# Time attention's scores in another order with the output behind them, and half of the band blocks whole

## The chip, the cores and the metric

The kernel runs on one core of one Trainium2 chip. The metric is the device time in microseconds (us). In the profile PE is TensorE's matmuls, PEld its weight loads, DVE VectorE, ACT ScalarE, POOL GpSimd, SP the engine that issues most DMAs.

## The reference, cut to what matters

```python
B, T, FB, C = (2, 256, 128, 128); H_T, H_F, BAND = (4, 4, 16)      # 4 heads of 32
xt = ln(x).transpose(0, 2, 1, 3)
x = x + mha(xt, t_wi, ..., causal_mask(T)).transpose(0, 2, 1, 3)   # over time
x = x + mha(ln(x), f_wi, ..., band_mask(FB, BAND))                 # over the 128 bands, |i - j| <= 16
x = x + gelu(ln(x) @ w1.T + b1) @ w2.T + b2                        # 128 -> 512 -> 128
# mha: softmax(q @ k.T / sqrt(32) + mask) @ v per head, then @ wo.T + bo
```

All in fp32, and each fp32 product (a matmul of the program) stands in the trace as two weight loads and two matmul records.

## The kernel before

**Tiling.** The work is cut into groups of four tiles of 128 rows by 128 channels: 128 groups `OverTime` (two sequences of 256 times each), then 128 `OverBands` (four times of 128 bands) and 128 `FeedForward`, in runs of eight of each in turn. Scores and weights are kept with keys on the partitions and queries along the free dimension. TensorE is used in tiles: `product` cuts a product of 128 columns into four of 32 columns (128\*32 in the profile), and scores use 32 rows (one head) by 64 columns (half of a tile's keys), 32\*64. There are so eight lanes (head, half) for scores and four column lanes for the rest.

**Order.** `run` walks over steps n and writes each engine's instructions in an order by hand; `InOrder` pins it. A step of the time stage holds pieces of several groups. On TensorE these are: the scores (`time_scores`), made up of the second tiles of group n (`second_scores`) and the first tiles of group n+1 (`first_scores`); `weigh` of group n-1, first the row sums rp (product with ones), then the weighted values op; `output` of group n-2 (yp = oT times the output weights); `queries_keys` and `values` of group n+2. ACT takes the exponentials of the scores (`second_weights`, `first_weights`) head by head, then `root_in_bank`, the two steps of `invert` on rp, two more exponentials, and copies q, k and v. DVE does `statistics`, `normalize` and `turn` (a 32x32 transpose, whose result goes through DRAM: four writes, `turned`, and one read a step later, `fetch`) of later groups, then `refine`, `finish` (adds yp to the residual, and issues the stores on SP at every second group) and `divide` (three instructions; the last makes oT). POOL masks and adds the weights.

**Banks.** [...] In the time stage they have names: first scores of head h go to a0 to a3, second scores to b0 to b3. When the exponentials have read them, the products of the same step take them: before, rp takes b0, op b3, yp a1, q a2, k b1 and v b2 (`Attention.place`, L1094). At the step's end the names are handed on in a cycle (L1167): of the banks just filled, a1 (yp) stays a1, b0 (rp) becomes a0, b1 (k) a3, and b3 (op) b1; q's stays a2 and v's b2. A score has to wait till the bank's last reader is done.

**Scores.** A first tile's keys face 256 queries; half 0 of them (e = 0) is multiplied with 256 columns, half 1 with 192 (the rest is masked). A second tile's keys face 128: 128 columns for one half and 64 for the other. The order before goes by pairs: for each (head, kind, sequence) both halves. The band scores (`OverBands.scores`) go block by block, half by half, head by head: 32 products of 64 keys by 80 queries a group.

Of the kernel before, what the change touches and what calls it, by code (L numbers as in the profile page):

```python
# [19 lines left out]
P = 128  # L20
H = 4
D = 32
BAND = 16
EPS = 1e-5
NEG = -1e38
NT = 4
# [6 lines left out]
HALF = P // 2  # L33
# [613 lines left out]
def rows_of(h):  # L647
    return slice(h * D, (h + 1) * D)
# [9 lines left out]
class OverTime(Attention):  # L658
# [16 lines left out]
        self.p1 = path.work.tile([P, 2, H, 2, P], F32, name="p1", tag="h", bufs=2)  # L675
        self.s1 = {h: path.bank([P, 2, P], "sp", path.banks[f"b{h}"]) for h in range(H)}

    def first_scores(self, h, s):
        r, a = rows_of(h), 2 * s * P
        for e in range(0, P, HALF):  # L680
            self.path.tensor.matmul(
                self.s0[h][e : e + HALF, s, e:], self.kT[r, a + e : a + e + HALF], self.qT[r, a + e : a + 2 * P],
                start=True, stop=True,
            )

    def second_scores(self, h, s):
        r, a = rows_of(h), (2 * s + 1) * P
        for e in range(0, P, HALF):
            q = P - HALF - e
            self.path.tensor.matmul(  # L690
                self.s1[h][e : e + HALF, s, q:], self.kT[r, a + q : a + q + HALF], self.qT[r, a + q : a + P],
                start=True, stop=True,
            )

    def first_weights(self, heads):
        for h in heads:
# [41 lines left out]
        self.rp = rp.rearrange("p s n q -> p (s n q)")  # L738


def time_scores(old, new):


    if new is not None:
        new.first_tiles()
    if old is not None:
        old.second_tiles()
    for h, second, s in (
        (0, 1, 0), (1, 0, 0), (2, 0, 0), (3, 1, 0), (0, 1, 1), (3, 1, 1), (0, 0, 0), (3, 0, 0),
        (1, 0, 1), (2, 0, 1), (0, 0, 1), (3, 0, 1), (1, 1, 0), (2, 1, 0), (1, 1, 1), (2, 1, 1),  # L750
    ):
        if second and old is not None:
            old.second_scores(h, s)
        if not second and new is not None:
            new.first_scores(h, s)


class OverBands(Attention):
# [5 lines left out]
    def scores(self, heads):  # L764
        path = self.path
        self.sp = {h: path.bank([P, NT * P], "sp") for h in heads}
        for i in range(NT):
            for e in range(2):
                keys = slice(e * HALF, (e + 1) * HALF)
                a = i * P + e * (HALF - BAND)  # L770
                q = slice(a, a + HALF + BAND)
                for h in heads:
                    r = rows_of(h)
                    path.tensor.matmul(
                        self.sp[h][keys, q], self.kT[r, i * P + e * HALF : i * P + (e + 1) * HALF], self.qT[r, q],
                        start=True, stop=True,
                    )

    def first_function(self):
# [107 lines left out]
class BoundedPath:  # L887
# [170 lines left out]
    def run(self, x, out):  # L1058
        groups = list(self.groups(x, out))

        def do(n, *names):
            if 0 <= n < len(groups):
                for name in names:
                    getattr(groups[n], name)()

        def at(n, kind):
            return 0 <= n < len(groups) and isinstance(groups[n], kind)

        def do_at(n, kind, *names):
            if at(n, kind):  # L1070
                do(n, *names)


        run0 = [i for i in range(len(groups)) if at(i, OverBands)][: RUN // NT]
        due = dict(zip(run0, (-5, -4, -4, -3, -1, 0, 1, 2)))
        due = {n: [i for i in run0 if run0[0] + due[i] == n] for n in range(-12, len(groups) + 2)}
        A = RUN // NT

        self.scalar.preload_act_table_set(EXP_SET)
        for n in range(-12, len(groups) + 2):  # L1080
            feeds = [at(n - 2 + i, FeedForward) for i in range(5)]
            bands = [at(n - 2 + i, OverBands) for i in range(5)]
            turn = feeds[2] and bands[1]
            old, new = (groups[i] if at(i, OverTime) else None for i in (n, n + 1))
            if bands[2] and feeds[1]:
                self.scalar.preload_act_table_set(EXP_SET)
            do_at(n + 4, FeedForward, "root")
            do(n, "first_half", "first_function", "first_mask")
            if n >= 0:
                do_at(n + 5, OverTime, "statistics")  # L1090
            if old is not None or new is not None:
                time_scores(old, new)
                b = self.banks
                Attention.place = dict(rp=b["b0"], op=b["b3"], yp=b["a1"], qp=b["a2"], kp=b["b1"], vp=b["b2"])  # L1094
            else:
                Attention.place = {}
            if old is not None:
                old.second_weights(old.late)
            if new is not None:
                new.first_weights(new.early[:1])  # L1100
            if old is not None:
                old.second_weights(old.early)
                old.mask_second()
                old.add(0)
                old.add(1)
            if new is not None:
                new.first_weights(new.early[1:])
            if n >= 0:
                do_at(n + 5, OverTime, "root_in_bank")
            if turn:  # L1110
                do(n, "second_half", "second_function")
            do_at(n + 3, OverTime, "fetch")
            do_at(n + 2, (OverBands, FeedForward), "fetch")

            for i in (2 * n + 12, 2 * n + 13) if n < -2 else (n + 10,) if n < 2 else ():
                if i >= NT:
                    do(i, "load")
            if n < -8 or n >= 0:
                do(n + 12, "load")
            if n >= 0:  # L1120
                for i in due[n]:
                    do(i, "statistics")
            do_at(n + 3, (OverBands, FeedForward), "normalize", "turn")
            do_at(n + 4, OverTime, "normalize", "turn")
            if n >= 0:
                do_at(n + 5, OverTime, "refine")
            if n < 0:
                do(n + 5, "statistics")
            do_at(n + 5, FeedForward, "statistics")
            if n == -4:  # L1130
                self.fold_rest()
                self.warm()
            do(n - 1, "weigh")
            do(n - 1, "invert_exactly" if turn else "invert")
            if new is not None:
                new.first_weights(new.late)
            if bands[2] or turn or old is not None:
                do(n - 2, "output", "finish")
            do(n - 1, "divide")
            if not turn:  # L1140
                do(n, "second_half", "second_function")
            if n in run0:
                do(n, "bias")
            if not bands[2] and old is None:
                do_at(n, FeedForward, "bias")
                do_at(n + A, OverBands, "bias")
                if at(n - 1, FeedForward) and at(n - 2, OverBands):
                    do_at(n + A - 1, OverBands, "statistics", "root")
                if not turn:
                    do_at(n + A, OverBands, "statistics", "root")  # L1150
            do_at(n + 2, OverTime, "queries_keys", "take_query", "take_key")
            do_at(n + 1, OverBands, "queries_keys", "take_query", "take_key")
            if n < 0:
                do_at(n + 5, OverTime, "root_by_scalar", "refine")
            for i in due[n]:
                do(i, "root_by_scalar", "refine")
            do_at(n, OverTime, "bias")
            if new is not None:
                new.mask_first()
            if not bands[2] and not turn and old is None:  # L1160
                do(n - 2, "output", "finish")
            do_at(n + 2, OverTime, "values", "take_values")
            do_at(n + 1, OverBands, "values", "take_values")
            if old is not None or new is not None:

                b = self.banks
                self.banks = dict(  # L1167
                    a1=b["a1"], a2=b["a2"], b0=b["a0"], b3=b["a3"], a0=b["b0"], a3=b["b1"], b1=b["b3"], b2=b["b2"]
                )


# [67 lines left out]
```

## Time and profile before

| | us |
|---|---|
| median of 3 runs (2706.91 to 2709.16) | 2707.29 |
| the profiled execution's own time | 2709.79 |
| its span | 2708.0 |
| busy PE / DVE / POOL / ACT in the span | 2670.3 / 2176.8 / 1952.8 / 1858.2 |

The span is the time from the first to the last instruction of the profiled execution. Busy time is the time in which at least one instruction of the engine is under way by its record; a matmul's end is modelled, so on PE the distance from start to start says more than busy time. In the lines of groups, the columns are: line, engine, operation, out<-in, tile rows\*columns, shape, count, then busy us, mean ns of one, idle us before it and who ended it. Every operation goes through one helper, so all have its line, L882. Timeline lines give the start, the duration, and the merged instructions.

The granted TensorE clock is full throughout. The time stage takes up the first 970 us or so, the bands and the feed-forward the rest.

### The profile page before, as it was taken

To read this page: it belongs to the slowest core of one execution; us is meant where nothing else is said; L and a number is where in the kernel's file an instruction comes from. 1 tells how busy PE (TensorE), PEld (TensorE's weight loads), DVE (VectorE), ACT (ScalarE), POOL (GpSimd) and SP (SyncE) were. 2 spreads that over 40 slices of the span, in tenths; PEclk is the share of its full clock that TensorE was granted. 3 is DMA by queue.
4 is the path that set the end of the run, shared out by engine and by line. 5 is a ranking of instruction groups with operands and counts; after the bars stand their busy time and mean duration, and the time that the engine had idled before them with its cause. 6 is when DMAs were issued, how large, how long until landed. Compare 5 with 4: busy or idle time off the path is not lost.

```text
span 2708.0 us, 156754 instructions
## 1 busy us (share of the span) xinstructions
PE 2670.3 (99%) x68662; PEld 1826.6 (67%) x68662; DVE 2176.8 (80%) x6708; ACT 1858.2 (69%) x3620; POOL 1952.8 (72%) x2297
## 2 busy tenths in 40 slices
PE   8999999999999999999999999999999999999998
PEld 5766666666766666666666666666666667666665
DVE  7888888888888898868779678687697796886974
ACT  6888888888888874755746647557456465575563
POOL 4888888888888887667657666676576666665762
PEclk9999999999999999999999999999999999999999
DMA  5555555555555535445454454454444444544533
GB/s 147 152 148 145 149 148 141 150 146 146 150 141 149 145 95 137 109 117 135 106 127 124 114 130 110 120 133 111 124 126 113 124 118 120 130 113 123 128 100 82
DMA packets 471513, 347.10 MB, mean 128 GB/s; under 512 B 43297, under 2 KB 405153, under 8 KB 470817
## 3 DMA queue, kind: packets, MB, share of 16 engines
q1 hardware_dynamic: 469568, 335.92, 48.2%
q8 instruction: 540, 8.85, 1.5%
q14 instruction: 157, 1.28, 0.2%
q10 hardware_dynamic: 1248, 1.05, 0.1%
HBM read 169.03 MB, written 167.77 MB: 124 GB/s over the span
## 4 chain that ended last, share of the span: by engine, by line
PE 81%; DVE 14%; DMA 2%; issue 1%; SPq 1%; ACT 0%; DVEq 0%; ACTq 0%
PE bank L882 81%; DVE xh L882 3%; DVE bank L882 3%; DVE z L882 2%; DVE stats L882 2%; DVE u L882 2%; DVE x L882 1%; DMA xnT<-turned 1%; DVE mv L882 1%; DMA turned<-z 1%; SPq L882 1%; DMA x<-in_x 0%; DVE oT L882 0%; DMA rows_sb<-in_rows 0%; ACT p L882 0%
## 5 line engine op out<-in xcount | busy, mean ns | idle before, releaser
L882 ACT ACTIVATE hT<-bank,b 128x512 f32<-128x512 f32 x512 | 347.0, 688 | 535.8 <-PE bank L882 517.7
L882 POOL TENSOR_SCALAR_AFFINE_SELECT pf<-pf 128x512 f32<-128x512 f32 x768 | 478.6, 637 | 248.1 <-ACT pf L882 221.7
L882 DVE TENSOR_SCALAR xh<-x,mv,rstd 128x160 f32<-128x160 f32 x1536 | 596.9, 431 | 14.3
L882 PEld LDWEIGHTS bank<-w2T_sb,hT 128*32 128x32 f32 x16384 | 459.7, 110 | 63.3 <-issue 39.7
L882 PE MATMUL bank<-xnT,wf 128*32 128x512 f32 x4096 | 489.1, 592 | 2.5 <-ACT p L882 2.5
L882 PE MATMUL bank<-w2T_sb,hT 128*32 128x128 f32 x16384 | 477.7, 273 | 1.1 <-issue 0.8
L882 PE MATMUL bank<-xnT,w1f 128*32 128x512 f32 x4096 | 474.8, 592 | 0.0
L882 DVE TENSOR_TENSOR res<-bank,res 128x512 f32<-128x512 f32 x256 | 175.9, 687 | 338.9 <-PE bank L882 337.7
L882 POOL TENSOR_SCALAR_AFFINE_SELECT p<-p 128x1024 f32<-128x1024 f32 (+2 forms) x384 | 364.8, 950 | 109.9 <-ACT p L882 101.4
L882 ACT ACTIVATE p<-bank 128x512 f32<-128x512 f32 (+1 forms) x1024 | 417.4, 499 | 21.7 <-PE bank L882 4.1
L882 PE MATMUL bank<-qT,kT 32*64 32x80 f32 (+4 forms) x16384 | 351.7, 274 | 3.7 <-DVE oT L882 2.4
L882 PEld LDWEIGHTS bank<-wf,xnT 128*32 128x32 f32 x8192 | 236.0, 110 | 153.9 <-issue 101.2
L882 PEld LDWEIGHTS bank<-qT,kT 32*64 32x64 f32 x16384 | 295.7, 130 | 58.9 <-ACT kT L882 48.0
L882 POOL TENSOR_TENSOR p<-p,p 128x512 f32<-128x512 f32 x256 | 324.1, 1287 | 10.7
L882 DVE BATCH_NORM_STATS2 stats<-x 128x6 f32<-128x128 f32 x1536 | 326.5, 275 | 0.6 <-DMA x<-in_x 0.6
L882 ACT ACTIVATE pf<-bank 128x512 f32<-128x512 f32 x512 | 267.0, 602 | 50.9 <-PE bank L882 48.9
L882 PEld LDWEIGHTS bank<-xnT,w1f 128*32 128x32 f32 x4096 | 156.4, 110 | 189.9 <-issue 160.3
L882 DVE STREAM_TRANSPOSE z<-xh 128x512 f32<-128x512 f32 x384 | 273.3, 712 | 13.5
L882 POOL TENSOR_SCALAR rstd<-mv 128x4 f32<-128x4 f32 x248 | 56.7, 229 | 311.7 <-DVE mv L882 310.3
L882 PE MATMUL bank<-wn,oT 128*32 128x128 f32 x8192 | 273.2, 273 | 0.0
L882 PE MATMUL bank<-wf,xnT 128*32 128x128 f32 x8192 | 273.0, 273 | 0.0
L882 POOL TENSOR_TENSOR rstd<-rstd,mhalf 128x4 f32<-128x4 f32 x248 | 257.0, 1036 | 20.7
(97 smaller groups left out, 3656.3 us busy)
## 6 DMA issues: line engine op xcount, KB each, us to landing
turned<-z SPq DMA_DIRECT2D x1536, 64.0 KB, 2.5
xnT<-turned SPq DMA_DIRECT2D x384, 256.0 KB, 3.2
x<-in_x SPq DMA_DIRECT2D x128, 256.0 KB, 4.4
x<-res SPq DMA_DIRECT2D x256, 128.0 KB, 2.4
x<-x SPq DMA_DIRECT2D x128, 256.0 KB, 4.3
out<-res SPq DMA_DIRECT2D x256, 128.0 KB, 2.5
w1T_sb<-in_w1T ACTq DMA_DIRECT2D x1, 256.0 KB, 6.6
w2T_sb<-in_w2T ACTq DMA_DIRECT2D x1, 256.0 KB, 8.0
```

What stands on the lines that cost most here:

```text
L882: return self.tc.keep_in_program_order(emit(*args, **kwargs))
```

## The change

Four things are done at once. `first_scores` and `second_scores` make one product instead of two, and `time_scores` goes through a list of the 32 products one by one. The names of the banks are given out otherwise: yp b0, rp b3, op a1; and the cycle at the step's end is another. In the time stage `output` of group n-2 is called right after the scores and the calls for the exponentials of b0 and b3, and `finish` between `normalize` and `turn`, with its stores ahead of `turn`'s writes on SP. In `OverBands.scores` blocks 1 and 2 are one product of 128 keys by 128 queries a head; blocks 0 and 3 stay as they were, so that a group has 24 products.

```diff
-    def first_scores(self, h, s):
+    def first_scores(self, h, s, e):
         r, a = rows_of(h), 2 * s * P
-        for e in range(0, P, HALF):
...
+        self.path.tensor.matmul(
+            self.s0[h][e : e + HALF, s, e:], self.kT[r, a + e : a + e + HALF], self.qT[r, a + e : a + 2 * P],
+            start=True, stop=True,
+        )
...
+TIME_ORDER = """
+    s000 s301 s011 s300 f101 f211 s100 s311 s010 s001 s111 f300 f110 f000 f210 f301
+    f201 f011 f200 f111 s310 f100 f010 f310 s211 f311 s201 f001 s110 s101 s210 s200
+""".split()
...
-    for h, second, s in (
-        (0, 1, 0), (1, 0, 0), (2, 0, 0), (3, 1, 0), (0, 1, 1), (3, 1, 1), (0, 0, 0), (3, 0, 0),
-        (1, 0, 1), (2, 0, 1), (0, 0, 1), (3, 0, 1), (1, 1, 0), (2, 1, 0), (1, 1, 1), (2, 1, 1),
-    ):
...
+    for kind, h, s, e in TIME_ORDER:
+        if kind == "s" and old is not None:
+            old.second_scores(int(h), int(s), int(e) * HALF)
+        if kind == "f" and new is not None:
+            new.first_scores(int(h), int(s), int(e) * HALF)
...
-        for i in range(NT):
-            for e in range(2):
-                keys = slice(e * HALF, (e + 1) * HALF)
-                a = i * P + e * (HALF - BAND)
-                q = slice(a, a + HALF + BAND)
+        for i, part in ((0, HALF), (1, P), (2, P), (3, HALF)):
+            reach = 0 if part == P else BAND
+            for e in range(0, P, part):
+                a = i * P + (e - reach if e else 0)
+                q, keys = slice(a, a + part + reach), slice(i * P + e, i * P + e + part)
                 for h in heads:
...
-                Attention.place = dict(rp=b["b0"], op=b["b3"], yp=b["a1"], qp=b["a2"], kp=b["b1"], vp=b["b2"])
+                Attention.place = dict(yp=b["b0"], rp=b["b3"], op=b["a1"], qp=b["a2"], kp=b["b1"], vp=b["b2"])
...
                 old.second_weights(old.late)
+                do(n - 2, "output")
...
-            do_at(n + 4, OverTime, "normalize", "turn")
+            do_at(n + 4, OverTime, "normalize")
+            if old is not None:
+                do(n - 2, "finish")
+            do_at(n + 4, OverTime, "turn")
...
-            if bands[2] or turn or old is not None:
+            if bands[2] or turn:
                 do(n - 2, "output", "finish")
...
-                    a1=b["a1"], a2=b["a2"], b0=b["a0"], b3=b["a3"], a0=b["b0"], a3=b["b1"], b1=b["b3"], b2=b["b2"]
+                    a1=b["b1"], a2=b["a2"], b0=b["a0"], b3=b["a3"], a0=b["b0"], a3=b["b3"], b1=b["a1"], b2=b["b2"]
```

In the list a name is kind (f first, s second), head, sequence, half.

More of the change, by code (lines that the diff above doesn't have):

```diff
@@ L676, in second_tiles, with second_scores @@
         self.s1 = {h: path.bank([P, 2, P], "sp", path.banks[f"b{h}"]) for h in range(H)}
-    def first_scores(self, h, s):
+    def first_scores(self, h, s, e):
         r, a = rows_of(h), 2 * s * P
-        for e in range(0, P, HALF):
[L681 to L693, printed above, removed]
+        self.path.tensor.matmul(
+            self.s0[h][e : e + HALF, s, e:], self.kT[r, a + e : a + e + HALF], self.qT[r, a + e : a + 2 * P],
+            start=True, stop=True,
+        )
+    def second_scores(self, h, s, e):
+        r, a, q = rows_of(h), (2 * s + 1) * P, P - HALF - e
+        self.path.tensor.matmul(
+            self.s1[h][e : e + HALF, s, q:], self.kT[r, a + q : a + q + HALF], self.qT[r, a + q : a + P],
+            start=True, stop=True,
+        )
     def first_weights(self, heads):
@@ L747, in time_scores @@
         old.second_tiles()
-    for h, second, s in (
-        (0, 1, 0), (1, 0, 0), (2, 0, 0), (3, 1, 0), (0, 1, 1), (3, 1, 1), (0, 0, 0), (3, 0, 0),
-        (1, 0, 1), (2, 0, 1), (0, 0, 1), (3, 0, 1), (1, 1, 0), (2, 1, 0), (1, 1, 1), (2, 1, 1),
-    ):
[L752 to L755, printed above, removed]
+    for kind, h, s, e in TIME_ORDER:
[3 more added lines that the diff above has]
+            new.first_scores(int(h), int(s), int(e) * HALF)
 class OverBands(Attention):
@@ L774, in scores @@
                     path.tensor.matmul(
-                        self.sp[h][keys, q], self.kT[r, i * P + e * HALF : i * P + (e + 1) * HALF], self.qT[r, q],
-                        start=True, stop=True,
+                        self.sp[h][e : e + part, q], self.kT[r, keys], self.qT[r, q], start=True, stop=True
                     )
```

## The prediction

> **What bounds the kernel now.** I read the page first: its busy times, then the chain that ended last.
>
> ```profile
> PE 2670.3 (99%) x68662; PEld 1826.6 (67%) x68662; DVE 2176.8 (80%) x6708; ACT 1858.2 (69%) x3620; POOL 1952.8 (72%) x2297
> PE 81%; DVE 14%; DMA 2%; issue 1%; SPq 1%; ACT 0%; DVEq 0%; ACTq 0%
> ```
>
> TensorE looks full and carries the chain. But matmul ends are modelled, so a full PE may hide poor use. The timeline of one time step (PE) shows where:
>
> ```profile
> 607.58 1.66 PE L882 MATMUL bank<-qT,kT 32*64 32x64 f32 x64
> 609.17 1.07 PE L882 MATMUL bank<-p,ones 128*32 128x256 f32 x16
> 610.06 1.48 PE L882 MATMUL bank<-p,v 128*32 128x256 f32 x32
> 611.36 1.06 PE L882 MATMUL bank<-wn,oT 128*32 128x128 f32 x32
> 612.23 1.90 PE L882 MATMUL bank<-xnT,wf 128*32 128x512 f32 x16
> 613.95 1.06 PE L882 MATMUL bank<-wf,xnT 128*32 128x128 f32 x32
> 614.93 0.45 PE L882 MATMUL bank<-qT,kT 32*64 32x64 f32 x8
> ```
>
> From start to start the step is 7.35 us: scores 1.59, row sums (rp) 0.89, weighted values (op) 1.30, output (yp) 0.87, queries and keys 1.72, values 0.98. The output's 16 fp32 products are 32 records of 128 columns in four column lanes, eight passes a lane: 0.109 us a pass. The others run at that rate too; only the scores do not. Their groups by shape:
>
> ```profile
> L882 PE MATMUL bank<-qT,kT 32*64 32x128 f32 x2048 | 199.2, 277 | 0.0
> L882 PE MATMUL bank<-qT,kT 32*64 32x256 f32 x2048 | 174.4, 386 | 0.0
> L882 PE MATMUL bank<-qT,kT 32*64 32x192 f32 x2048 | 168.9, 331 | 0.0
> ...
> L882 PE MATMUL bank<-qT,kT 32*64 32x80 f32 x8192 | 137.9, 244 | 1.6 <-DVE x L882 1.0 <-DVE oT L882 0.4 <-ACT kT L882 0.2
> ...
> L882 PE MATMUL bank<-qT,kT 32*64 32x64 f32 x2048 | 115.0, 223 | 2.1 <-DVE oT L882 2.1
> ```
>
> A 64-column record costs 56 ns of busy time (115.0/2048), a 256-column one 85. Eight lanes (four heads by two key halves) stand open. Start-to-start times within one lane are 0.058, 0.109, 0.1625 and 0.216 us for a pass of 64, 128, 192 and 256 columns. Each lane of half 0 has four passes of 256 and four of 64 (1.10 us), each of half 1 four of 192 and four of 128 (1.09). The scores stream for 1.50 us (607.583 to 609.082), so 0.4 us is lost.
>
> The single records tell why. The first 17 products stand ready; the 18th, 19th and 20th load weights 0.355, 0.466 and 0.686 us after the first, each 0.03 after the (modelled) ends of products 1, 2 and 3, at 0.325, 0.436 and 0.655. [...] Lane (2,1) sits idle from 0.41 to 0.69 us as its next product is the 20th. Filled in by this rule, the lanes of before end at 1.495 us; 1.499 is measured.
>
> The weight loads around the scores show the second cost:
>
> ```profile
> 607.14 0.24 PEld L882 LDWEIGHTS bank<-wf,xnT 128*32 128x32 f32 x8
> 607.58 1.42 PEld L882 LDWEIGHTS bank<-qT,kT 32*64 32x64 f32 x64 [0.20 <-ACT kT L882]
> 609.17 0.16 PEld L882 LDWEIGHTS bank<-p,ones 128*32 128x32 f32 x8 [0.17 <-issue]
> ```
>
> The last score pass starts at 608.973 and streams 0.109: the next shape's load comes 0.087 later. The lanes of half 0 were empty from 608.8, and still nothing of the new shape loaded. At nearly every change between these shapes the gap is 0.088 to 0.094 us, and 128\*128 to 128\*32 (columns alone) took 0.094.
>
> [...] In the trace a first pass is late by 29 ns with 32 columns and 48 with 64, so about 0.1 us for 128 is my estimate.
>
> **The change, part by part.** T is the first score load of a step.
>
> *Score order.* The same 32 products in another order, nothing added. By the rule above: lane (2,1) gets its products 6th, 17th, 25th and 27th[...]. All lanes end at 1.24 us. One wait is new: bank b2 (25th product, due at 0.68) is free only when ACT has copied v,
>
> ```profile
> 607.72 0.59 ACT L882 COPY v<-bank 128x512 f32<-128x512 f32 x1 [0.28 <-PE bank L882]
> 608.45 2.19 ACT L882 ACTIVATE p<-bank 128x256 f32<-128x256 f32 x6
> ...
> 614.20 0.59 ACT L882 COPY kT<-bank 128x512 f32<-128x512 f32 x1 [0.17 <-PE bank L882]
> ```
>
> ending at T+0.73, seen at 0.79; the seven products behind it wait too: 1.28. Before, b2 came 27th, when it was free. Lane (2,0) starts with the 15th product, which must pass seven blocked ones; the trace shows two passed. If it can't, it starts 0.14 later: 1.38. Gain 0.22 to 0.12; I take 0.20 for 127 steps: **-25 us**.
>
> *Outputs behind the scores, banks.* The same 32 records, moved. yp takes b0: its exp ends at T+1.25 (608.84), and yp begins at 1.28+0.09: covered. Its oT is done at the last step's divide. rp takes b3, whose last score is now the 21st (T+1.2), so exps 2 to 6 come 0.11 later, the reciprocal ends at T+4.73 for 4.62, divide at 6.93. The op bank (a1, next step's b1) is wanted by the 7th product at 7.13+0.04: 0.2 to spare. kT's bank is wanted by the 5th: ACT frees it about then, 0 to 0.05 us. DVE had slack,
>
> ```profile
> 612.54 0.69 DVE L882 TENSOR_TENSOR res<-bank,res 128x512 f32<-128x512 f32 x1 [0.87 <-PE bank L882]
> ```
>
> and finish now waits for yp until T+2.5, so the transpose behind it starts at 3.11 for 2.95. On SP every second step's four stores (0.48 us each) now go ahead of the four turned writes, so the next fetch waits about 1 us more; its xnT is wanted over 5 us later. POOL (6.7 us busy a step) keeps 0.3 us. **0 us**, from -2 to +10.
>
> *Band blocks.* A band group's scores now:
>
> ```profile
> 1430.07 1.06 PE L882 MATMUL bank<-qT,kT 32*64 32x80 f32 x64
> 1431.07 1.06 PE L882 MATMUL bank<-pf,ones 128*32 128x512 f32 x8
> ...
> 1436.40 1.04 PE L882 MATMUL bank<-qT,kT 32*64 32x80 f32 x64
> ```
>
> They stream 0.905 us, then 0.087 of change. After: block 0 in halves, 0.05 start + 2 passes of 0.069 + 7 issues of 0.0066 = 0.235; change 0.09; blocks 1 and 2 whole in four lanes, 0.1 + 4 × 0.109 + 0.02 = 0.56; change 0.09; block 3, 0.235. Sum 1.21: 0.29 more, and each group of this stage has TensorE full from start to start, so nothing hides it. Over 128 groups **+37 us**. Both ends: a first pass late by only 0.05 makes it +30; if the two shapes run side by side without a drain, the lanes end at 0.81 and it is -12. I take the drain, as every shape change traced pays it.
>
> **Sum.** -25 + 0 + 37 = +12 on the profiled execution's 2709.8 us, whose span is 2708.0; it stands 2.5 above the median of 2707.3, so against that I forecast 2719.
>
> **Rivals.** (1) *No drain between 32\*64 and 32\*128*, since the row tile stays: -25 - 12 = -37, 2670 us. For it: only products with the same 32 rows meet. Against: a pure column change drained. It decides the sign: with less than 25/128 = 0.2 us lost a group, in place of 0.29, the change is faster. (2) *The time stage gains nothing*: lane (2,0), b2 and kT together, or a divide chain 0.2 us late, hold the 7th product and all behind it; then 0 + 37: 2744. Against: 0.2 us to spare on that chain. (3) *The order works, and a step turns to ACT or POOL as bound*: these need 6.6 to 6.7 us against 7.13, so it takes nothing yet.
>
> **Numbers.** Forecast 0.56, rival 1 0.32, rival 2 and the like 0.12. The forecast's own range is 2704 to 2734: 13 to 33 gained, 30 to 40 lost. From 2668 to 2738 I hold 8 in 10. About 0.2% (5.4 us) can be told from no change. Faster: nearly all of rival 1 and a tenth of the forecast, 0.36; same: 0.17; slower: most of the forecast and rival 2, 0.47.
>
> **What will show it.** In the time step: scores start to start 1.37 (right) or 1.5 and more; p,ones after wn; step 7.13. In a band group: three score runs with 0.09 us between last pass and next load, start to start about 1.3, not 1.0. One unbroken run of mixed shapes in 0.9 us would make the forecast wrong.

## The result, and the profile after

The changed kernel takes 2718.27 us in the median of seven runs (2715.07 to 2720.52), the kernel before 2707.58 beside it: ratio 1.0034, interval 1.0025 to 1.0044. It is slower by 0.34%, about 10.7 us, which the runs can tell from no change. The profiled executions' spans are 2715.7 and 2708.0 us, at mean granted clocks of 0.998 and 0.999. One execution of the experiments below (`order_only`, 3106.0 us at a granted clock of 0.828) was slow and is left out of the figures.

The page of the kernel after, its busy times and its chain:

```profile
PE 2687.0 (99%) x66614; PEld 1817.2 (67%) x66614; DVE 2181.6 (80%) x6708; ACT 1854.8 (68%) x3620; POOL 1947.9 (72%) x2297
PE 86%; DVE 11%; DMA 1%; issue 0%; ACT 0%; POOL 0%; SPq 0%; DVEq 0%; POOLq 0%; ACTq 0%
```

TensorE runs 2048 records fewer and is busy for longer: as a count of work the change looks like a gain, and it is a loss. DVE, ACT and POOL move by under 5 us each. The time stage and the bands are read apart here, since the change aims at a gain in one and touches the other. A time step of the kernel after, PE alone:

```profile
610.58 1.48 PE L881 MATMUL bank<-qT,kT 32*64 32x64 f32 x64
611.99 1.08 PE L881 MATMUL bank<-wn,oT 128*32 128x128 f32 x32
612.88 1.05 PE L881 MATMUL bank<-p,ones 128*32 128x256 f32 x16
613.75 1.48 PE L881 MATMUL bank<-p,v 128*32 128x256 f32 x32
```

The output (wn,oT) now stands behind the scores, and the scores take 1.40 us from start to start, for 1.59 before. The rest of the step takes on PE what it took before, and the step goes from 7.352 to 7.168 us (medians of some 120 steps each). The band scores of one group are seen best in the weight loads, looked at in four stretches of time:

```profile
1429.92 0.23 PEld L881 LDWEIGHTS bank<-qT,kT 32*64 32x64 f32 x16 [0.20 <-ACT kT L881]
1430.25 0.54 PEld L881 LDWEIGHTS bank<-qT,kT 32*128 32x128 f32 x16
1430.90 0.23 PEld L881 LDWEIGHTS bank<-qT,kT 32*64 32x64 f32 x16
1431.23 0.16 PEld L881 LDWEIGHTS bank<-pf,ones 128*32 128x32 f32 x8
```

Block 0 in halves, blocks 1 and 2 whole, block 3 in halves, and the next product: 0.32, 0.66 and 0.32 us, 1.305 in all for 0.994 before. A pass is one matmul record on one lane; its stream is taken as the time from start to start of two passes on one lane. The last pass of block 0 starts at 1430.092 and streams 0.069 to 1430.161; the first whole block's load comes 0.087 later. The prediction and the expectations call this gap the drain. Over all groups it is 0.086 to 0.088 us from 32\*64 to 32\*128 (128 times) and 0.089 to 0.090 us back (128 times), with 0.069 us for a pass of 80 columns and 0.109 for one of 128.

The balance of the two spans: the first band scores start at 957.6 us for 976.8, 19.2 us gained in the time stage; from there to the end it takes 1758.1 us for 1731.1, 26.9 lost. Together +7.7; the medians are 10.7 apart, as the profiled execution before lies 2.2 above its median and the one after 0.8 below.

### The profile page after: what moved, and what is told of

Its sections match the earlier page's. It is cut to its first block, busy times and chain, and to the rows that moved or that the text cites. A ratio compares the mean times of both kernels' runs of the same rounds, so it can differ in the third digit from the quotient of the medians.

```text
span 2715.7 us, 152631 instructions
## 1 busy us (share of the span) xinstructions
PE 2687.0 (99%) x66614; PEld 1817.2 (67%) x66614; DVE 2181.6 (80%) x6708; ACT 1854.8 (68%) x3620; POOL 1947.9 (72%) x2297
## 3 DMA queue, kind: packets, MB, share of 16 engines
q14 instruction: 156, 1.28, 0.2%
## 4 chain that ended last, share of the span: by engine, by line
PE 86%; DVE 11%; DMA 1%; issue 0%; ACT 0%; POOL 0%; SPq 0%; DVEq 0%; POOLq 0%; ACTq 0%
PE bank L881 86%; DVE xh L881 2%; DVE bank L881 2%; DVE stats L881 1%; DVE u L881 1%; DVE z L881 1%; DVE x L881 1%; DVE oT L881 1%; DMA xnT<-turned 1%; DVE mv L881 1%; DMA x<-in_x 0%; POOL p L881 0%; POOL pf L881 0%; DMA rows_sb<-in_rows 0%; DMA turned<-z 0%
## 5 line engine op out<-in xcount | busy, mean ns | idle before, releaser
L881 ACT ACTIVATE p<-bank 128x512 f32<-128x512 f32 (+1 forms) x1024 | 430.5, 495 | 30.6 <-PE bank L881 4.6
L881 PE MATMUL bank<-qT,kT 32*64 32x80 f32 (+5 forms) x14336 | 368.2, 288 | 3.6 <-DVE oT L881 2.2
L881 PEld LDWEIGHTS bank<-qT,kT 32*64 32x64 f32 (+1 forms) x14336 | 300.5, 138 | 84.4 <-ACT kT L881 48.8
L881 POOL TENSOR_TENSOR p<-p,p 128x512 f32<-128x512 f32 x256 | 324.1, 1288 | 10.7
L881 PEld LDWEIGHTS bank<-xnT,w1f 128*32 128x32 f32 x4096 | 150.5, 110 | 193.9 <-issue 169.0
```

The source lines that it names most:

```text
L881: return self.tc.keep_in_program_order(emit(*args, **kwargs))
```

## The experiments

All ratios are to the kernel before in the same set of runs, with 95% intervals.

**The two parts alone.** `bands_only` is the kernel before with the new `OverBands.scores`:

```diff
-        for i in range(NT):
-            for e in range(2):
+        for i, part in ((0, HALF), (1, P), (2, P), (3, HALF)):
...
```

> Kernel before with the band blocks of the change alone. If the two changes of tile shape cost what the trace of the change shows (1.305 us a group from score start to the next product, for 0.994 before) and part of it is taken back at the turn of each run: time stage unchanged at 7.35 us a step, +27 us, 2734 us. If the change's loss came from elsewhere, in the time stage, and the band blocks cost little: within 5 us of before.

Measured: 2735.94 us, ratio 1.0099 (1.0083 to 1.0116), 28 us more than before. The step stays at 7.353, the band scores are at 1.305. `time_only` is the change with all blocks in halves:

```diff
-        for i, part in ((0, HALF), (1, P), (2, P), (3, HALF)):
+        for i, part in ((0, HALF), (1, HALF), (2, HALF), (3, HALF)):
```

> The change with all four band blocks in halves again, as before. If the two parts add up: time step 7.17 us as in the changed kernel, band scores at 0.99 us a group, 2688 us, 19 us under before. If the time part gains only where the bands give it back (the stages meet in one pipeline), or its gain is an accident of that run: 2700 us or more.

Measured: 2691.38 us, ratio 0.9943 (0.9926 to 0.9959), 16.5 us less; its span is 19.3 us shorter. The step is 7.168, the band scores 0.995. So the parts add up within their intervals: 28.0 - 16.5 = 11.5 us, for 10.7 measured of both. The loss is the bands' alone.

**Is it the change of shape, or the whole block?** All three kernels have the change's time part and vary the blocks. `all_whole` has none of the changes of shape inside a group:

```diff
+        for i, part in ((0, P), (1, P), (2, P), (3, P)):
```

> The change's time part with all four band blocks whole: 16 products a group, one tile shape, no change of shape inside the group. If the changes of shape are the cost: 0.1 fill + 8 passes of 0.109 + 0.02 + 0.09 for the one change that stays = 1.08 us a group, +8 to +11 us on time_only, some 2697 us, faster than the change. If the whole block itself is dear (0.15 us each over two halves): 1.6 us a group and 2740 us or more.

Measured: 2696.82 us, ratio 0.9958 (0.9942 to 0.9975). Four whole blocks are cheaper than two, though still dearer than all halves: 5.4 us more than `time_only`, for the 8 to 11 expected. Its PE timeline shows 1.10 us from the scores to the next product:

```profile
1433.51 1.17 PE L881 MATMUL bank<-qT,kT 32*128 32x128 f32 x32
1434.62 1.06 PE L881 MATMUL bank<-pf,ones 128*32 128x512 f32 x8
```

`grouped` keeps the 24 products and has one change inside:

```diff
+        for i, part in ((0, HALF), (3, HALF), (1, P), (2, P)):
```

> The change with the two half blocks first and then the two whole ones: the same 24 products with one change of shape inside the group in place of two. If each change is a drain of 0.09 us and a fill of 0.05: 16 products in halves end at 0.40 us, then 0.09 + 0.1 + 0.436 + 0.02 + 0.09, 1.13 us a group for 1.305, 2702 us. If the order of the blocks doesn't matter, since the whole blocks are the cost: 1.3 us a group and 2718 us as the change.

Measured: 2700.73 us, ratio 0.9966 (0.9952 to 0.998); 1.119 us a group in the median. One group:

```profile
1429.79 1.19 PE L881 MATMUL bank<-qT,kT 32*64 32x80 f32 x48
1430.91 0.64 PE L881 MATMUL bank<-pf,ones 128*32 128x512 f32 x4
```

`alternate` has three:

```diff
+        for i, part in ((0, HALF), (1, P), (2, HALF), (3, P)):
```

> The change with the blocks half, whole, half, whole: again two whole blocks and 24 products a group, but three changes of shape inside it in place of two. If each change costs a drain and a fill: 0.235 + 0.09 + 0.34 + 0.09 + 0.235 + 0.09 + 0.34 + 0.09 = 1.50 us from the group's score start to the next product, for 1.305 in the change, 25 us more less what the turn of each run takes back: 2735 to 2743 us. If two whole blocks cost the same wherever they stand: 1.3 us and 2718 us.

Measured: 2744.57 us, ratio 1.0133 (1.0116 to 1.015), a shade over the range that was expected; 1.515 us a group in the median, 1.51 in this one:

```profile
1439.48 1.58 PE L881 MATMUL bank<-qT,kT 32*64 32x80 f32 x48
1440.99 0.64 PE L881 MATMUL bank<-pf,ones 128*32 128x512 f32 x4
```

The same 24 products thus take 1.119, 1.305 and 1.515 us with one, two and three changes: 0.186 us for the second and 0.21 for the third. The prediction's terms, which the trace of the kernel after shows one by one, give just that. The second brings one more run of halves: a gap of 0.09, a fill (the time by which a first pass is late) of 0.05, and 0.046 for eight lanes that start 6.6 ns after one another. The third brings one more run of whole blocks: 0.09, a fill of 0.1, and 0.02 for four lanes.

From the first band scores to the end of the span it is 1730.9 us in `time_only`, 1737.2 in `all_whole`, 1737.5 in `grouped`, 1758.1 in the kernel after and 1781.9 in `alternate`. With no change inside a group four whole blocks cost little over halves, so the whole block as the culprit falls.

**What carries the time part's gain?** `order_only` is the kernel before with `TIME_ORDER` alone:

```diff
-    for h, second, s in (
-        (0, 1, 0), (1, 0, 0), (2, 0, 0), (3, 1, 0), ...
+    for kind, h, s, e in TIME_ORDER:
```

> Kernel before with the new score order alone: output, banks and bands as before. The order takes bank b1 with the 7th product, and in the old cycle that bank is op of the step before, which divide frees only about 0.4 us after the scores start. If the order needs the other banks: the 7th product and all behind it stand till 0.42 us, the scores stream 1.57 us for 1.50, the step is 7.4 us, 2712 to 2718 us. If the order alone carries the gain and the banks are free enough: 1.32 us of scores, 7.17 us a step, 2688 us.

Measured: 2726.79 us, ratio 1.0071 (1.0051 to 1.0091); slower, and by more than expected: the scores took 1.63 us of stream for 1.57 and the step 7.48 for 7.4. Where these further 0.06 us come from was not followed. The 7th product's load, the first on bank b1, comes 0.420 us after the first. The timeline of PE, and the wait in a stretch of 400 us:

```profile
609.10 1.78 PE L882 MATMUL bank<-qT,kT 32*64 32x64 f32 x64
610.81 0.42 PE L882 MATMUL bank<-p,ones 128*32 128x256 f32 x4
```

```profile
PEld bank L882 <- DVE oT L882: 10.3, 52, 0.2
```

So the steps (52 waits in 400 us) wait for divide (oT) to let go of op's bank; in the same stretch the kernel after has no such entry. `output_banks` has the move and the cycle with the old order:

```diff
 TIME_ORDER = """
-    s000 s301 s011 s300 f101 f211 ...
+    s000 s001 f100 f101 f200 f201 s300 s301 s010 s011 s310 s311 f000 f001 f300 f301
+    f110 f111 f210 f211 f010 f011 f310 f311 s100 s101 s200 s201 s110 s111 s210 s211
```

> The output behind the scores and the other bank cycle, with the old order of scores (written out product by product) and all band blocks in halves. If the move itself brings nothing and only makes room for the order: scores 1.52 to 1.58 us of stream (the third product now waits for k's bank, 0.04 to 0.1 us), step 7.35 to 7.43 us, 2705 to 2718 us. If the move carries the gain (a wait on PE that the profile hid): step near 7.2 us and 2690 us.

Measured: 2708.47 us, ratio 1.0001 (0.9992 to 1.001); scores 1.588 and step 7.352 us in the median, as before. The expected wait for k's bank did not show. The move and the banks bring nothing without the order, the order costs 19 us without them, and together they gain 16.5. The wait in `order_only` is for a bank, so it is by the banks that the new names and cycle make room for the order; whether they would do so with the output left in its old place was not run.

**Does the rule for the order hold?** The rule is the author's estimate. It is worked out from the trace of before, where the 18th, 19th and 20th products load 0.03 us after the (modelled) ends of the 1st, 2nd and 3rd, and from the traced times of the passes. In the kernel after, the 15th product loads at 0.171 us, 0.001 after the 8th, while three earlier products (the 10th, 11th and 14th) still wait; so the full rule lets a product pass three waiting ones at most. `tuned` is `time_only` with a third order, laid out by this full rule:

```diff
 TIME_ORDER = """
+    s310 s300 s001 s311 s010 f211 f101 s000 s011 f110 s301 f210 f111 s100 f201 f200
+    f000 f310 f100 f001 f311 f011 f300 f301 s101 f010 s201 s211 s210 s110 s111 s200
```

> time_only with a third order of the same 32 products, laid out by the rule read from the trace of before [...]: long products on every lane early, b2 last. If the rule holds: stream 1.28 us for 1.32, the step 7.13 us for 7.17, 5 us under time_only, 2683 us. If the order matters in another way than by the rule: 1.35 to 1.6 us of scores and 2690 to 2730 us.

Measured: 2682.78 us, ratio 0.991 (0.9893 to 0.9927). It beats both kernels, and `time_only` by some 8.6 us in the medians, 3 more than expected. In the traces the 126 intervals between full steps carry 5.5 us of it, as the rule has it; the rest lies at the two ends of the stage. These vary: in the five executions with the change's time part the first band scores start at 954.2 to 963.2 us. Its steps:

```profile
605.67 1.43 PE L881 MATMUL bank<-qT,kT 32*64 32x64 f32 x64
607.03 1.08 PE L881 MATMUL bank<-wn,oT 128*32 128x128 f32 x32
```

Scores 1.358 us from start to start (1.28 + 0.087 = 1.365 by the rule), the step 7.122 us for 7.13. This is the one order whose time the full rule gave ahead of its run; the rule is not shown beyond these orders.

## Why the prediction was right, and where it was off

2719 was forecast and 2718.3 measured, by the likeliest case. Both its terms have the right sign and both are too large, so that the total is as close as that is luck. Step by step:

- *The gap at a change of shape.* Right. The trace of before had no change from 32\*64 to 32\*128, so that the 0.09 us taken for it was the author's estimate from the other changes; 0.086 to 0.090 was measured. The three stretches of a group were forecast at 0.325, 0.65 and 0.325 us and measured at 0.32, 0.66 and 0.32. The fill of a 128-column load, an estimate at 0.1 from those of 32 and 64 columns, is about that: the first whole pass takes 0.213 us to the next, the later ones 0.112 (the forecast had 0.109). For 32 columns the forecast read 29 ns; from the first pass to the second it is 24, and nothing hangs on it. One sum is off: 1.21 less 0.905 is 0.305, not 0.29, so its own lines give 39 us for 128 groups, and the scores did take 38.7 us more. Rival 1 falls.
- *"Nothing hides it."* This step failed. The scores take 38.7 us more over 128 groups (0.302 each in the mean), but the stage only 26.9. PE's row sums of the bands, in the list by shape, before and then after, with the idle time before them:

```profile
L882 PE MATMUL bank<-pf,ones 128*32 128x512 f32 x1024 | 137.1, 604 | 12.0 <-DVE u L882 12.0
```

```profile
L881 PE MATMUL bank<-pf,ones 128*32 128x512 f32 x1024 | 136.4, 604 | 2.9 <-DVE u L881 1.5
```

  Before, once in each of the 16 runs, at the turn from bands to feed-forward, the row sums of the last band group waited up to 0.8 us for DVE's divide of the group before. The end of one run shows why:

```profile
1448.87 0.69 DVE L882 TENSOR_TENSOR bank<-bank,r 128x512 f32<-128x512 f32 x1
1455.39 0.69 DVE L882 TENSOR_TENSOR bank<-bank,r 128x512 f32<-128x512 f32 x1
1461.93 0.69 DVE L882 TENSOR_TENSOR bank<-bank,r 128x512 f32<-128x512 f32 x1
1463.49 1.06 PE L882 MATMUL bank<-pf,ones 128*32 128x512 f32 x8 [0.80 <-DVE u L882]
```

  In these groups the timeline marks no idle time on DVE, which comes round every 6.53 us, while PE takes 6.33 us a group (1430.07 to 1436.40 in the prediction's lines). PE looks full, but DVE falls behind by 0.2 us a group, and PE waits for it at the turn. In the kernel after PE takes 6.64 us a group and DVE keeps up. From the first feed-forward product to those row sums it is 4.37 us before and 3.79 after in the mean, 9.1 us over the 16 turns; the other 2.6 us or so that did not show were not traced. The other kernels agree: the wait for u is 12.2 us in `time_only`, with the old band scores, 7.9 in `all_whole` and 6.7 in `grouped` (6.44 and 6.45 us a group on PE in the median), and 0.6 in `bands_only` and in `alternate` (6.64 and 6.85). The 12.0 us stood in the list of PE's groups from which the forecast quotes the scores, and it passed over them.
- *The score order.* The estimate from the load times had the right sign, and its size was a little too good. The 25th product's wait for b2 was due at 0.79 us and comes at 0.775. The 15th product was to start 0.14 us late if it can't pass the blocked ones, that is at 0.23 in place of 0.09; it came at 0.17, when the 8th had loaded and three earlier ones still waited. The scores stream 1.317 us, between the two ends given (1.28 and 1.38). With at most three waiting products passed, the limit read from this same trace, the rule gives 1.319. The gain is 0.184 us a step for the 0.20 taken, and 19.2 us for 25 over the stage: 127 steps would make 23.4, and some 4 us go in the pipeline's first steps and its end, which the forecast counted as steps.
- *Output, finish and banks.* Right at 0 us: `output_banks` differs from before by 0.4. Two waits that were foreseen stand in DVE's timeline of the kernel after:

```profile
613.23 0.69 DVE L881 TENSOR_TENSOR res<-bank,res 128x512 f32<-128x512 f32 x1 [0.30 <-PE bank L881]
613.84 0.70 DVE L881 STREAM_TRANSPOSE z<-xh 128x512 f32<-128x512 f32 x1
...
615.40 0.70 DVE L881 TENSOR_TENSOR bank<-bank,r 128x512 f32<-128x512 f32 x1 [0.43 <-ACT r L881]
```

  Finish waits 0.30 us for yp, for 0.87 before, and the transpose starts at T+3.26 (3.11 was forecast); divide now waits 0.43 us for ACT's reciprocal, and its last instruction ends at T+7.04 (6.93). Bank b1 is wanted at 7.168 + 0.04. About 0.17 us is left there before PE would wait, an estimate from these figures.

Two terms were too large: 6 us of gain that did not come, and 10 us of loss that was hidden. They have opposite signs and in part cancelled: the traces differ by 7.7 us for the 12 forecast, and the medians by 10.7. Rivals 2 and 3 do not hold: the step did gain, and ACT and POOL do not hold it up.

## What to carry to other kernels

Fewer products are not less time where tile shapes alternate: count the changes of shape, here 0.19 to 0.21 us for one more in a group, and put all products of one shape side by side. Here even that did not beat the old halves (1.119 us a group for 0.995). An engine that is full from start to start may still run ahead of a slower one and pay for it at the end of the stage, here up to 0.80 us at the turn of a run and 12.0 us over the 16 runs: set their times per group side by side. For small products on many lanes try other orders: here the same 32 products streamed for 1.499, 1.317 and 1.264 us, the last with long products early on every lane, and those whose bank is freed last at the end. A move that brings nothing alone may be what an order needs: see what bank each early product takes, and who frees it.

## What the runs showed of the hardware

- Between the tile shapes 32\*64, 32\*128 and 128\*32, nearly every change in the traces of before and after took 0.086 to 0.092 us from the end of the last pass's stream to the next load; the one change from 128\*128 to 128\*32 took 0.091, for the 0.094 in the prediction. Then comes a fill, read in the kernel after from the first pass to the second on its lane, less a pass: 0.024, 0.05 and 0.10 us for loads of 32, 64 and 128 columns.
- fp32 products on tiles did not start in the program's order across lanes: in the kernel after the 15th product, on an empty lane, started 0.172 us after the first load, ahead of the 12th at 0.186. In the trace of before the 18th, 19th and 20th products loaded at 0.355, 0.466 and 0.686 us, 0.03 after the (modelled) ends of the 1st, 2nd and 3rd. The rule, the author's estimate from these times, gave the scores' stream as 1.495, 1.319 and 1.277 us for three orders; 1.499, 1.317 and 1.264 were measured. The first two were worked out from traces in hand, the third ahead of its run.
- The products behind one that waited for its bank, on other lanes too, loaded after it: in the kernel after the 25th product, which waits for b2, loads at 0.775 us, and the seven behind it from 0.78 us on; in `order_only` the 7th product held up the rest until 0.420 us.
